# A four-layer graph network on one core: earlier loads at the end of layer 0, and layer 3's W2 products in pairs of 64 rows with the bias written by ScalarE

## The chip, the core and the metric

The kernel runs on one core of one Trainium2 chip, as one launch. The metric is the device time of one execution in microseconds; several executions are timed, and the median is given. The engines are TensorE (PE, with its weight loads PEld), VectorE (DVE), ScalarE (ACT), GpSimd (POOL) and SyncE (SP). SP issues the ordinary DMA transfers, POOL the indirect ones (gathers).

## What is computed

There are 8192 nodes with 32 features, and 262144 edges, sorted by target. Four layers follow each other, each one `x = layernorm(x + layer(x))`.

```
layer 0: w_e = weight[edge_type]            # 64 relations, 32x32 each
         out = segment_sum(x[src] @ w_e, dst)
layer 1: out = segment_sum(x[src] * edge_weight, dst)
layer 2: out = segment_sum(x[src], dst)
layer 3: h = relu(edge_attr_32 @ W1 + b1)   # 64 wide
         w = (h @ W2 + b2).reshape(E, 4, 8, 8)
         messages from x[src], edge_attr_4 and w, then segment_sum over dst,
         plus a product of each node's own x with si_w0 and si_w1
```

## The kernel before

The order of every engine's work is written out by hand in `raw_layers`. A `Flow` wraps an engine; `X.after(marks)` makes engine X wait for marks of other engines, `X.mark(ins)` makes one. All engines work in their program order, so an instruction that waits holds up all that stands behind it on its engine.

**Layer 0** walks over 256 groups `g` of eight tiles of 128 edges. POOL gathers rows of a table of products (`fetch_rows`, line 454), 12 groups ahead of their use and held to PE's marks; DVE splits the rows into three bf16 parts (`parts`, 806 to 811); PE adds them up by one-hot matrices (845). Beside it the loop does work for later layers. `matrices` builds 256 pieces of the dense matrices of layers 1 and 2 (PE line 654, in pairs of 64 rows; ACT 658 and 659) and stores them to DRAM (`amat` for layer 1, `cmat`, one byte per count, for layer 2). The last piece is made at group 207. `layer1(g)` multiplies such matrix pieces, loaded again by SP (`load1`, 695), with the node blocks that layer 0 has normalized already (715). A plan places 224 of the 256 products of layer 1 beside layer 0. The 32 that need the last block of nodes are left for layer 1's tail.

**Layer 1's tail** runs over `c` from 0 to 31: eight matmuls on a matrix piece of 1 MB (715), ACT's copy (724), a turn back by a small product (937), and a normalization for every fourth `c`. There are six buffers for the pieces. `pump` loads three of the 32 before layer 0 ends; the other loads wait for the end of layer 0 or for a buffer. The first 4 MB of layer 2's counts (`bring(0)`, 886) are loaded behind the first loads of the tail, and `widen(0, range(3))` turns them to bf16 at c = 16, split over DVE, ACT and POOL (965).

**Layer 2** has 16 such pieces of counts, each with 64 matmuls (1009).

**Layer 3** walks over 512 quads `q` of four tiles. POOL gathers four tiles per quad from the table `xtab`, eight quads ahead: `fetch_rows(q + AHEAD)` waits for the W2 products of quad q. Once for every two quads, `hidden(q + 2)` makes `h` for both: two matmuls with 32 rows of weights (1146), and two ACT instructions with Relu, one for each quad (1154), to a buffer of 65 rows whose last row is one. Then PE makes the W2 products of quad q (1170, 65 rows, so that the bias comes with the product) into one of two PSUM buffers, and then the sums of quad q - 4 (1179). DVE multiplies w with the gathered rows (1207, 1210, 1214), and its last product frees the PSUM buffer (`w_free`). So PE's order for two quads is: hidden, W2, sums, W2, sums.

Of the kernel before, what the change touches and what calls it, by code (L numbers as in the profile page):

```python
# [13 lines left out]
BF = mybir.dt.bfloat16  # L14
I32 = mybir.dt.int32
AF = mybir.ActivationFunctionType
# [5 lines left out]
P = 128  # L22
N = 8192
E = 262144
D = 32
# [10 lines left out]
GG = TT // GT  # L36
# [112 lines left out]
CB = 256  # L149
# [4 lines left out]
NC1 = 32  # L154
# [3 lines left out]
U8 = mybir.dt.uint8  # L158
# [45 lines left out]
def raw_layers(tc, x, a, w0, w1, b1, w2, si, m, bad):  # L204
    nc = tc.nc
    PE, V, A, G, S = (Flow(tc, e, n) for e, n in ((nc.tensor, "pe"), (nc.vector, "dve"), (nc.scalar, "act"),
                                                  (nc.gpsimd, "pool"), (nc.sync, "sp")))
# [32 lines left out]
    def now(f):  # L240
        return (f.sem, f.n)
# [9 lines left out]
    cut = Carve()  # L251
# [430 lines left out]
    def slot_of(n):  # L682

        r = n - n_in
        if r < 3:
            return 3 + n % 3, n - 3
        order = [3 + (n_in + k) % 3 for k in range(3)] + [0, 1, 2]
        return order[r % 6], (n - 6 if r >= 6 else None)

    def load1(n, *more):  # L690

        c, z = items[n]
        k, before = slot_of(n)
        S.after(stored[8 * c + 6], stored[8 * c + 7], used1.get(before), *more)
        land1[n] = m_ld[k].add(S.e.dma_start(slot1[k], amat[c // 16][c % 16, z, 0:P * 2048].rearrange("(p w) -> p w", w=2048)))

    def pump():

        while loaded[0] < len(items) and loaded[0] < n_in + 3:
            n = loaded[0]  # L700
            c, z = items[n]
            if made < 8 * (c + 1) or (n >= 3 and n - 3 not in used1):
                break
            load1(n)
            loaded[0] += 1

    def products(n, acc, first, last):
# [47 lines left out]
    def layer1(g):  # L755
# [11 lines left out]
            turned.append((c, h, h, take(sums1[:, h], bank[:, 6, 256 * h:256 * (h + 1)], pm, sums1_free[h])))  # L767
        pump()


    NS = TT // WT
    NO = 4
# [53 lines left out]
    for g in range(GG + 2):  # L826
        if g >= 2 and (g - 2) % per == per - 1:
            vm = bank_out((g - 2) // per)
            while done < NB // LC and ready(done) <= g - 1:
                acc = bank[:, (g - 2) // per % 2, 0:LC * D]  # L830
                agg_free[(g - 2) // per % 2] = vm = normalize(0, done, acc, windows(done, acc, (vm,)), x_a, x_b)
                normed[done] = ln_last[0]
                done += 1
        if g >= GG:
            continue
        h, bk, c = g % NO, (g // per) % 2, g % per
        if g == FIRST // 2:
            V.after(slots(), x_in)
        V.after(oh_free[h])
        pairs(oh[:, h], P, rel_b[:, g * GT:(g + 1) * GT])  # L840
        PE.after(parts(g))
        if c == 0:
            PE.after(agg_free[bk])
        for t in range(GT):
            ins = PE.e.matmul(bank[:, bk, 3 * c * D:3 * (c + 1) * D], oh[:, h, t // 2, :, t % 2],  # L845
                              xp[:, g % 4, t].rearrange("p c f -> p (c f)"), start=(t == 0), stop=(t == GT - 1))
        oh_free[h] = sums_of[g] = PE.mark(ins)
        turn_back()
        fetch_rows(g + AHEAD, 0, sums_of[g])
        if g >= FIRST:  # L850
            upto = min(CB, (g - FIRST + 1) * CB // SP1)
            while made < upto:
                matrices(made)
                made += 1
        add_up()
        fetch_rows(g + AHEAD, 1, now(PE))
        layer1(g)


    cut = Carve(33792)  # L860
    x3 = cut(NB, 3 * D, dt=BF)
    sums = cut(2, 512)
# [10 lines left out]
    for c in range(NC1):  # L873
        if c not in begun1:
            V.e.memset(y1[:, 2 * c:2 * c + 2, :], 0.0)
    cast = {}
    c_ld = [Landing(tc, f"ld_cm{k}") for k in range(2)]
    land = {}

    u8 = [arena[:, k:k + 8192].bitcast(U8) for k in (0, 16384)]  # L880
    ring = [arena[:, k:k + 4096].bitcast(BF) for k in (8192, 12288, 29696, 24576)]

    def bring(c, *free):
        if c < 16:
            S.after(*(cast[c - 2][-1] if c >= 2 else free))
            land[32 + c] = c_ld[c % 2].add(S.e.dma_start(u8[c % 2].rearrange("p (i w) -> p i w", w=2048),
                                                         cmat[16 * c:16 * (c + 1)].rearrange("i p w -> p i w")))

    while loaded[0] < min(len(items), n_in + 6):
        load1(loaded[0], *end)  # L890
        loaded[0] += 1
    bring(0, *end)
    G.after(*end)
    PE.after(ln_last[0], acc_free[0])
    sum_bank = [None, None]
# [50 lines left out]
                normed2[c * nb // LC] = ln_last[0]  # L946

    normed2 = {}
    ring_free = [None] * 4
    SHARE = (0, 48, 104, 128)  # L950

    def widen(c, ks=range(4)):

        if c >= 16:
            return
        cast.setdefault(c, [])
        v = u8[c % 2].rearrange("p (u r) -> p u r", r=256)
        for k in ks:
            o = ring[k].rearrange("p (u r) -> p u r", r=64)
            ms = []  # L960
            for e, F in enumerate((V, A, G)):
                us = slice(SHARE[e], SHARE[e + 1])
                F.after(land[32 + c], ring_free[k])
                src_, dst_ = v[:, us, 64 * k:64 * (k + 1)], o[:, us, :]
                ms.append(F.mark(F.e.activation(dst_, src_, AF.Copy) if F is A else F.e.tensor_copy(dst_, src_)))  # L965
            cast[c].append(ms)

    n = n_in
    for c in range(NC1):
        b = c % 2  # L970
        PE.after(sum_bank[b])
        for e in range(got[c], NQ1):
            pm = products(n, bank[:, b, 0:256], e == got[c], e == NQ1 - 1)
            if n + 6 < len(items):
                load1(n + 6)
            n += 1
        sum_bank[b] = am = take(sums[:, b, 0:256], bank[:, b, 0:256], pm, sum_free[b])
        if pend:
            turn(*pend)
        pend = (1, c, c, am)  # L980
        if c == NC1 // 2:
            widen(0, range(3))
    bring(1, pm)
    turn(*pend)
    ring_free[3] = pm
# [50 lines left out]
    w1_s = cut(64)  # L1036
    b1_s = cut(1)
    w2_s = cut(256)
    hs = cut(4, 512)
    ef = cut(3, 2, 512)  # L1040
    sh = cut(3, WT, 4)
    a0 = cut(2, WT, 16)
# [19 lines left out]
        c_ld.add(S.e.dma_start(w1_s[q * D:(q + 1) * D, :], w1))  # L1062
    for h in range(2):
        c_ld.add(S.e.dma_start(b1_s[64 * h:64 * h + 64], b1))
    c_in = c_ld.add(S.e.dma_start(w2_s[0:65], w2))
    for k in range(4):
        hm = V.mark(V.e.memset(hs[64:65, k], 1.0))

    e_ld = [Landing(tc, f"ld_ef{k}") for k in range(3)]
    s_ld = [Landing(tc, f"ld_sh{k}") for k in range(3)]  # L1070
# [50 lines left out]
    fetch(2)  # L1121
    PE.after(*free)
    A.after(*free)
    A.after(c_in, hm)

    h_free = None
    w_free = [zf[0], zf[1]]
# [11 lines left out]
    def hidden(q):  # L1139

        s = q // 8
        k = s % 3
        PE.after(batch[s]["e"], quad.get(q - 1, {}).get("h", h_free))
        for h in range(2):
            r = q % 4 + h
            ins = PE.e.matmul(bank[64 * h:64 * h + 64, 2, :], w1_s[r * D:(r + 1) * D, :],  # L1146
                              ef[r * D:(r + 1) * D, k, (q % 8) // 4, :], start=True, stop=True,
                              tile_position=(r * D, 64 * h))
        pm = PE.mark(ins)
        if q % 8 == 6:  # L1150
            ef_free[k] = pm
        for h in range(2):
            A.after(pm, quad.get(q + h - 4, {}).get("w"))
            quad[q + h] = dict(h=A.mark(A.e.activation(hs[0:64, (q + h) % 4], bank[64 * h:64 * h + 64, 2, :], AF.Relu,  # L1154
                                                       bias=b1_s[64 * h:64 * h + 64])))

    for q in range(AHEAD):
        fetch_rows(q)
    factors(0)
    PE.after(c_in, *zf)  # L1160
    hidden(0)
    for q in range(NQ + LAG3 + 2):

        if q % 2 == 0 and q + 2 < NQ:
            hidden(q + 2)
        if q < NQ:
            k, wp = w_bank()
            PE.after(quad[q]["h"], w_free[k])
            for t in range(4):
                ins = PE.e.matmul(wp[:, t, :], hs[0:65, q % 4, t * P:(t + 1) * P], w2_s[0:65], start=True, stop=True)  # L1170
            quad[q]["w"] = PE.mark(ins)
            quad[q]["k"] = k, wp
            fetch_rows(q + AHEAD)
# [58 lines left out]
        if 0 <= c < NQ and c % 2 == 1:  # L1232
            g = c // 2
            V.after(quad[c]["a"])
            V.e.tensor_reduce(win[:, g, 0:8], bank[:, g % 2, 0:128].rearrange("p (o k) -> p o k", k=16), AX.X, OP.add)
            rm = V.mark(V.e.tensor_reduce(r1, bank[:, g % 2, 128:320].rearrange("p (mo i) -> p mo i", i=8), AX.X, OP.add))
            V.after(rm)
            gm = V.mark(V.e.tensor_tensor(win[:, g, 8:].rearrange("p (o m) -> p o m", m=3),
                                          bank[:, g % 2, 320:344].rearrange("p (o m) -> p o m", m=3),
                                          r1.rearrange("p (m o) -> p o m", o=8), op=OP.add))  # L1240
            agg_free[g % 2] = gm
            while done < NB // LC and ready(done) <= g + 1:
                k, wp = w_bank()
                acc = bank[:, 3 + 2 * k, 0:LC * D]
                w_free[k] = normalize(3, done, acc, windows(done, acc, (w_free[k], gm)), z, x_a)
                done += 1


# [469 lines left out]
```

## Time and profile before

| | |
|---|---|
| median of 11 runs | 5797.4 us (5791.28 to 5806.86) |
| the profiled execution, its own time | 5799.02 us |
| its span from first to last instruction | 5797.3 us |
| mean granted TensorE clock | 0.886 |
| busy share PE, DVE, ACT, POOL | 82%, 76%, 33%, 71% |
| layer 0's last gather ends | 2805.0 us |
| layer 1's tail, first product to last turn | 2819.1 to 2923.3 us |
| layer 2's products | 2929.2 to 3172.9 us |
| layer 3's first gather starts, last gather ends | 3181.6 us, 5752.8 us |

The span holds almost the whole of the time. Its two long stages are layer 0 and layer 3; between them lie 377 us from the last gather of the one to the first of the other. Busy time is a mean over stages of different kinds, so each stage is read by itself. The granted clock is 1.00 or 0.50 in any short stretch; a mean between them is a mixture.

### The profile page before, as it was taken

The numbers are of one execution on the slowest core, as the hardware profiler recorded it, in microseconds if no ns is written. First come the engines' busy times: TensorE is split into PE (matmuls) and PEld (weight loads), VectorE is DVE, ScalarE is ACT, GpSimd is POOL, SyncE is SP. The second block draws the span as 40 slices with busy tenths as digits, with TensorE's granted clock in tenths as the row PEclk, the third lists the DMA queues.
The fourth block names the chain that finished last, engine by engine and source line by source line (L and its number), as shares of the span: only waits on it lengthen the run. The fifth ranks groups of instructions, "written<-read, shape, count | busy, mean of one in ns | idle before, by whom it ended". The sixth has DMA issues, their size and how long they took to land.

```text
span 5797.3 us, 89080 instructions
## 1 busy us (share of the span) xinstructions
PE 4730.8 (82%) x34726; PEld 3367.2 (58%) x34726; DVE 4411.4 (76%) x9512; ACT 1887.1 (33%) x3061; POOL 4142.1 (71%) x4238
## 2 busy tenths in 40 slices
PE   7456777777777787734499999999999999999998
PEld 3156666666666666522255566666666666666665
DVE  4269898989989898543356788888888878888886
ACT  5265555555555555200177111111111111111110
POOL 2677777777777777777256777777777777777775
PEclk7568888989999899756589899999999999999999
DMA  9636666769789899935576111111111111111111
GB/s 350 214 109 198 189 211 223 252 228 322 252 295 319 274 351 326 353 119 183 219 259 220 25 29 30 26 30 30 26 30 26 30 30 26 30 26 30 26 30 22
DMA packets 583102, 865.29 MB, mean 149 GB/s; under 512 B 102605, under 2 KB 441614, under 8 KB 549134
## 3 DMA queue, kind: packets, MB, share of 16 engines
q1 hardware_dynamic: 448094, 782.68, 38.3%
q0 software_dynamic: 134144, 73.67, 6.6%
q8 instruction: 275, 4.51, 0.3%
q10 hardware_dynamic: 432, 3.15, 0.2%
q14 instruction: 157, 1.29, 0.1%
HBM read 454.28 MB, written 404.88 MB: 148 GB/s over the span
## 4 chain that ended last, share of the span: by engine, by line
PE 25%; POOL 12%; DMA 6%; issue 4%; DVE 4%; ACT 0%; POOLq 0%; SPq 0%; DVEq 0%
POOL f_arena L454 12%; PE bank L1179 10%; PE bank L1170 8%; DMA f_arena<-fxtab,f_src 6%; PE bank L1009 4%; PE bank L1146 2%; DVE f_arena L1214 1%; PE bank L575 1%; PE bank L715 1%; PE bank L937 1%; DVE f_arena L1210 0%; DVE f_arena L588 0%; DMA f_arena<-famat 0%; DVE f_arena L1112 0%; DVE f_arena L1110 0%
## 5 line engine op out<-in xcount | busy, mean ns | idle before, releaser
L454 POOL DMA_INDIRECT f_arena<-fytab,f_row x2048 | 1957.7, 956 | 652.4 <-issue 541.0
L454 POOL DMA_INDIRECT f_arena<-fxtab,f_src x2048 | 1947.4, 951 | 643.6 <-issue 522.3
L654 PE MATMUL bank<-f_arena 64*128 64x128 f32 x16384 | 1196.7, 303 | 405.8 <-DVE f_arena L643 277.5
L654 PEld LDWEIGHTS bank<-f_arena 64*128 64x128 f32 x16384 | 1101.3, 210 | 485.8 <-DVE f_arena L643 304.4
L1179 PE MATMUL bank<-f_arena 128*128 128x344 f32 x4096 | 1309.6, 462 | 0.0
L1170 PE MATMUL bank<-f_arena 65*128 65x256 f32 x4096 | 1019.5, 392 | 68.3 <-DVE f_arena L1214 68.1
L1154 ACT ACTIVATE f_arena<-bank,f_arena 64x512 f32<-64x512 f32 x512 | 350.8, 685 | 2109.6 <-PE bank L1146 2103.2
L1170 PEld LDWEIGHTS bank<-f_arena 65*128 65x128 f32 x4096 | 768.3, 193 | 420.1 <-DVE f_arena L1214 127.5
L1179 PEld LDWEIGHTS bank<-f_arena 128*128 128x128 f32 x4096 | 798.1, 195 | 358.3 <-issue 29.6
L658 ACT ACTIVATE f_arena<-bank 128x512 uint8<-128x512 f32 x1024 | 613.1, 599 | 840.3 <-PE bank L654 729.6
L659 ACT ACTIVATE f_arena<-bank 128x512 f32<-128x512 f32 x1024 | 611.9, 598 | 0.0
L640 DVE TENSOR_TENSOR f_arena<-bank,f_arena 128x2048 f32<-128x2048 bf16 x256 | 586.5, 2291 | 8.7
L1214 DVE TENSOR_TENSOR f_arena<-bank,f_arena 128x256 f32<-128x256 f32 x1536 | 553.0, 418 | 0.0
L845 PE MATMUL bank<-f_arena 128*128 128x96 bf16 x2048 | 152.2, 226 | 335.2 <-DVE f_arena L811 335.1
L1110 DVE TENSOR_TENSOR f_arena<-f_arena 128x192 f32<-128x192 f32 x256 | 92.2, 360 | 396.5 <-DMA f_arena<-fxtab,f_src 394.2
L715 PE MATMUL bank<-f_arena,f_x_b 128*32 128x256 f32 x4096 | 314.3, 447 | 74.5 <-DMA f_arena<-famat 56.8
L845 PEld LDWEIGHTS bank<-f_arena 128*128 128x128 bf16 x2048 | 110.9, 108 | 417.8 <-DVE f_arena L811 330.5
L1210 DVE TENSOR_TENSOR f_arena<-bank,f_arena 128x512 f32<-128x512 f32 x512 | 349.8, 683 | 0.0
L588 DVE TENSOR_TENSOR f_arena<-bank,f_rel 128x512 f32<-128x512 f32 x512 | 349.3, 682 | 0.0
L638 DVE TENSOR_TENSOR f_arena<-bank,f_arena 128x1024 f32<-128x1024 bf16 x256 | 312.3, 1220 | 14.1 <-PE bank L654 11.9
L643 DVE TENSOR_TENSOR f_arena<-f_arena,bank 128x1024 f32<-128x1024 f32 x256 | 309.8, 1210 | 0.0
L965 POOL CAST f_arena<-f_arena 128x1536 bf16<-128x1536 uint8 x64 | 169.0, 2654 | 187.8 <-PE bank L715 75.9
(146 smaller groups left out, 4427.1 us busy)
## 6 DMA issues: line engine op xcount, KB each, us to landing
famat<-f_arena SPq DMA_DIRECT2D x256, 1024.0 KB
f_arena<-famat SPq DMA_DIRECT2D x256, 1024.0 KB, 11.7
fytab<-f_arena SPq DMA_DIRECT2D x64, 1024.0 KB, 11.9
fcmat<-f_arena SPq DMA_DIRECT2D x256, 256.0 KB
f_arena<-fcmat SPq DMA_DIRECT2D x16, 4096.0 KB, 14.8
f_arena<-fytab,f_row POOLq DMA_INDIRECT x2048
f_arena<-fxtab,f_src POOLq DMA_INDIRECT x2048
f_arena<-laid_ea SPq DMA_DIRECT2D x64, 512.0 KB, 3.5
```

Source lines behind the costliest of these rows:

```text
L454: return G.e.indirect_dma_start(out=dest, out_offset=None, in_=table, in_offset=bass.IndirectOffsetOnAxis(ap=ix, axis=0))
L588: return V.e.tensor_tensor(o, iota[:, None, :].to_broadcast([P, n, P]), rel[:, t:t + n, None].to_broadcast([P, n, P]), op=OP.is_equal)
L640: V.e.tensor_tensor(oh_l[:, b], iota2[:, None, :, 0].to_broadcast([P, 16, P]), meta_l[:, pp, k0:k0 + 16, None].to_broadcast([P, 16, P]), o ...
L654: ins = PE.e.matmul(two[:, h].rearrange("p (c s j) -> p c s j", s=64, j=4)[:, :, :, j], oh_l[hs_, b, 4 * q + j, :], oh_k[hs_, b, 4 * q + j ...
L658: A.e.activation(st_c[:, b, q], two[:, :, 0:256], AF.Copy)
L659: pair_free[u] = am = A.mark(A.e.activation(st_a[:, b, :, q].rearrange("p z h w -> p h z w"), two[:, :, 256:512].rearrange("p h (z w) -> p ...
L715: ins = PE.e.matmul(acc[q * D:(q + 1) * D, :].rearrange("p (u h j) -> p u h j", h=2, j=4), x_b[:, 8 * z + s, :], mv[:, s], start=(first an ...
L1154: quad[q + h] = dict(h=A.mark(A.e.activation(hs[0:64, (q + h) % 4], bank[64 * h:64 * h + 64, 2, :], AF.Relu, bias=b1_s[64 * h:64 * h + 64])))
L1170: ins = PE.e.matmul(wp[:, t, :], hs[0:65, q % 4, t * P:(t + 1) * P], w2_s[0:65], start=True, stop=True)
L1179: ins = PE.e.matmul(bank[:, g % 2, 0:MW], oh[:, c % NO, t, :], p[:, c % NP, t, :], start=(c % 2 == 0 and t == 0), stop=(c % 2 == 1 and t = ...
L1210: V.e.tensor_tensor(pq[:, :, 0:128].rearrange("p t (o k) -> p t o k", k=16), wp[:, :, 0:128].rearrange("p t (o k) -> p t o k", k=16), a0[: ...
L1214: ins = V.e.tensor_tensor(pq[:, :, 128 + 64 * mm:192 + 64 * mm].rearrange("p t (o i) -> p t o i", i=8), wp[:, :, 192:256].rearrange("p t ( ...
```

## The change

The change has two parts.

**Loads moved into layer 0.** When the last piece of the matrices is made (group 207), two of the tail's pieces are loaded into buffers 0 and 1, which `matrices` has used until then, and `bring(0)` loads the first counts into buffers that are dead as well. `pump` may now load five of the tail's pieces before the end of layer 0, the other three in the buffers of the planned ones. From four groups later on, eight ACT copies, one per group, turn two of the four parts of the first counts to bf16. A third part is done at c = 0 of the tail by the three engines together, in place of all three at c = 16; the fourth stays where it was.

**Layer 3's W2 products.** `h` now has both quads side by side on 2 x 64 partitions, made by one ACT instruction; W2 lies twice, on partitions 0 to 63 and 64 to 127, and each quad's four products run in an order that alternates the two halves. The bias row is gone: for each quad ACT writes the bias into the PSUM buffer first, as soon as DVE has freed it, and the products add to it. Identity products of the bias (`written`) are new too: four at the beginning of layer 3, and one behind each of the eight window sums, ahead of its normalization.

```diff
     def slot_of(n):
         r = n - n_in
-        if r < 3:
+        if r < 0:
             return 3 + n % 3, n - 3
-        order = [3 + (n_in + k) % 3 for k in range(3)] + [0, 1, 2]
-        return order[r % 6], (n - 6 if r >= 6 else None)
+        order = [0, 1] + [3 + (n_in + k) % 3 for k in range(3)] + [2]
+        return order[r % 6], n - 6 if r >= 6 else n - 5 if 2 <= r < 5 else None
...
+    def early_counts(g):
+        k = g - soon[0]
+        if k == 0:
+            ring_free[0] = ring_free[1] = now(PE)
+            for n in (n_in, n_in + 1):
+                load1(n, stored[CB - 2], stored[CB - 1])
+            bring(0, now(V), stored[CB - 1])
+        elif 4 <= k < 12:
+            q, u = (k - 4) // 4, slice((k - 4) % 4 * 32, (k - 4) % 4 * 32 + 32)
+            A.after(land[32], ring_free[q])
+            am = A.mark(A.e.activation(ring[q].rearrange("p (u r) -> p u r", r=64)[:, u],
+                                       u8[0].rearrange("p (u r) -> p u r", r=256)[:, u, 64 * q:64 * (q + 1)], AF.Copy))
...
         layer1(g)
+        if made == CB and soon[0] is None:
+            soon[0] = g
+        if soon[0] is not None:
+            early_counts(g)
...
     while loaded[0] < min(len(items), n_in + 6):
         load1(loaded[0], *end)
         loaded[0] += 1
-    bring(0, *end)
...
-        if c == NC1 // 2:
-            widen(0, range(3))
+        if c == 0:
+            widen(0, [2])
...
-    c_in = c_ld.add(S.e.dma_start(w2_s[0:65], w2))
-    for k in range(4):
-        hm = V.mark(V.e.memset(hs[64:65, k], 1.0))
+        c_ld.add(S.e.dma_start(w2_s[64 * h:64 * h + 64], w2[0:64, :]))
+    c_in = c_ld.add(S.e.dma_start(b2_s, w2[64:65, :].to_broadcast([P, 256])))
...
-        for h in range(2):
-            A.after(pm, quad.get(q + h - 4, {}).get("w"))
-            quad[q + h] = dict(h=A.mark(A.e.activation(hs[0:64, (q + h) % 4], bank[64 * h:64 * h + 64, 2, :], AF.Relu,
-                                                       bias=b1_s[64 * h:64 * h + 64])))
+        A.after(pm, quad.get(q - 3, {}).get("w"))
+        hm = A.mark(A.e.activation(hs[:, q // 2 % 2], bank[:, 2, :], AF.Relu, bias=b1_s))
+        quad[q] = dict(h=hm)
+        quad[q + 1] = dict(h=hm)
+
+    def written(b, c0):
+        return PE.e.matmul(bank[:, b, c0:512].rearrange("p (r c) -> p r c", c=256), ident,
+                           b2_s[:, None, :].to_broadcast([P, 2 - c0 // 256, 256]), start=(c0 == 0), stop=True,
+                           skip_group_check=True)
+
+    def biases(k, wp):
+        A.after(w_free[k])
+        return A.mark(A.e.activation(wp, b2_s[:, None, :].to_broadcast([P, 4, 256]), AF.Copy))
...
         if q % 2 == 0 and q + 2 < NQ:
             hidden(q + 2)
         if q < NQ:
             k, wp = w_bank()
-            PE.after(quad[q]["h"], w_free[k])
-            for t in range(4):
-                ins = PE.e.matmul(wp[:, t, :], hs[0:65, q % 4, t * P:(t + 1) * P], w2_s[0:65], start=True, stop=True)
+            PE.after(quad[q]["h"], biases(k, wp))
+            for t in (0, 2, 1, 3):
+                hp, c0 = slice(32 * (t & 2), 32 * (t & 2) + 64), 256 * (q % 2) + t % 2 * P
+                ins = PE.e.matmul(wp[:, t, :], hs[hp, q // 2 % 2, c0:c0 + P], w2_s[hp], start=False, stop=True,
+                                  skip_group_check=True)
...
-                w_free[k] = normalize(3, done, acc, windows(done, acc, (w_free[k], gm)), z, x_a)
+                windows(done, acc, (w_free[k], gm))
+                w_free[k] = normalize(3, done, acc, PE.mark(written(3 + 2 * k, 256)), z, x_a)
```

The host lays `edge_attr_32` out in another order to match.

More of the change, by code (lines that the diff above doesn't have):

```diff
@@ L697, in pump @@
     def pump():
-        while loaded[0] < len(items) and loaded[0] < n_in + 3:
+        while loaded[0] < n_in + 5:
             n = loaded[0]
             c, z = items[n]
-            if made < 8 * (c + 1) or (n >= 3 and n - 3 not in used1):
+            before = slot_of(n)[1]
+            if made < 8 * (c + 1) or (before is not None and before >= 0 and before not in used1):
                 break
-            load1(n)
+            if n not in land1:
+                load1(n)
             loaded[0] += 1
@@ L768, in layer1, with bring, widen @@
         pump()
+    cast = {}
+    c_ld = [Landing(tc, f"ld_cm{k}") for k in range(2)]
+    land = {}
+    u8 = [arena[:, k:k + 8192].bitcast(U8) for k in (0, 16384)]
+    ring = [arena[:, k:k + 4096].bitcast(BF) for k in (8192, 12288, 29696, 24576)]
+    def bring(c, *free):
+        if c < 16:
+            S.after(*(cast[c - 2][-1] if c >= 2 else free))
+            land[32 + c] = c_ld[c % 2].add(S.e.dma_start(u8[c % 2].rearrange("p (i w) -> p i w", w=2048),
+                                                         cmat[16 * c:16 * (c + 1)].rearrange("i p w -> p i w")))
+    ring_free = [None] * 4
+    SHARE = (0, 48, 104, 128)
+    def widen(c, ks=range(4)):
+        if c >= 16:
+            return
+        cast.setdefault(c, [])
+        v = u8[c % 2].rearrange("p (u r) -> p u r", r=256)
+        for k in ks:
+            o = ring[k].rearrange("p (u r) -> p u r", r=64)
+            ms = []
+            for e, F in enumerate((V, A, G)):
+                us = slice(SHARE[e], SHARE[e + 1])
+                F.after(land[32 + c], ring_free[k])
+                src_, dst_ = v[:, us, 64 * k:64 * (k + 1)], o[:, us, :]
+                ms.append(F.mark(F.e.activation(dst_, src_, AF.Copy) if F is A else F.e.tensor_copy(dst_, src_)))
+            cast[c].append(ms)
+    def early_counts(g):
[10 more added lines that the diff above has]
+                                       u8[0].rearrange("p (u r) -> p u r", r=256)[:, u, 64 * q:64 * (q + 1)], AF.Copy))
+            if k % 4 == 3:
+                cast.setdefault(0, []).append([am])
+    soon = [None]
     NS = TT // WT
@@ L857, in raw_layers @@
         layer1(g)
+        if made == CB and soon[0] is None:
+            soon[0] = g
+        if soon[0] is not None:
+            early_counts(g)
+    assert soon[0] + 12 < GG
     cut = Carve(33792)
@@ L875, in raw_layers @@
             V.e.memset(y1[:, 2 * c:2 * c + 2, :], 0.0)
[L876 to L887, printed above, removed]
     while loaded[0] < min(len(items), n_in + 6):
@@ L948, in raw_layers @@
     normed2 = {}
[L949 to L966, printed above, removed]
     n = n_in
@@ L1038, in raw_layers @@
     w2_s = cut(256)
-    hs = cut(4, 512)
+    b2_s = cut(256)
+    hs = cut(2, 512)
     ef = cut(3, 2, 512)
@@ L1123, in raw_layers @@
     A.after(*free)
-    A.after(c_in, hm)
+    A.after(c_in)
     h_free = None
@@ L1161, in raw_layers @@
     hidden(0)
+    for b in range(3, 7):
+        ins = written(b, 0)
+    w_free[:] = [PE.mark(ins)] * 2
     for q in range(NQ + LAG3 + 2):
@@ L1704 @@
     laid["ea4"] = arrays["ea4"].reshape(TT, P, 4).transpose(1, 0, 2).reshape(P, TT * 4)
-    laid["ea32"] = arrays["ea32"].reshape(P, 4, 512, D).transpose(1, 3, 0, 2).reshape(P, P, 512)
+    laid["ea32"] = arrays["ea32"].reshape(P, 2, 2, 2, 256, D).transpose(1, 3, 5, 0, 2, 4).reshape(P, P, 512)
     arrays = {f"in_{k}": np.ascontiguousarray(v) for k, v in arrays.items()}
```

## The prediction

> **What bounds the kernel now.** I read the page's costliest groups first, then the chain of waits between the layers, then PE's timeline and the granted clock in layer 3.
>
> The groups (line, engine, shapes, count; then busy time, mean ns, idle time before):
>
> ```profile
> L454 POOL DMA_INDIRECT f_arena<-fxtab,f_src x2048 | 1947.4, 951 | 643.6 <-issue 522.3
> L1179 PE MATMUL bank<-f_arena 128*128 128x344 f32 x4096 | 1309.6, 462 | 0.0
> L1170 PE MATMUL bank<-f_arena 65*128 65x256 f32 x4096 | 1019.5, 392 | 68.3 <-DVE f_arena L1214 68.1
> ```
>
> Layer 3's 2048 gathers run from 3181.6 to 5752.8 us: 1.2555 us each, busy 0.95 and a gap of 0.30 that is there with nobody to wait for. So POOL bounds layer 3: two quads (eight gathers) take 10.04 us. Layer 0's gathers run the same way, so work added or moved inside layer 0 costs nothing until PE falls 12 groups behind.
>
> The chain between the layers (start, duration, what):
>
> ```profile
> 2819.42 8.40 DMA f_arena<-famat
> 2833.61 10.17 DMA f_arena<-famat
> 2874.57 9.24 ACT f_arena L965 x3
> ```
>
> PE waits in layer 1's tail for matrix loads that start late, and for ACT while it widens counts.
>
> PE's timeline in layer 3, two rounds of two quads, the first with a wait:
>
> ```profile
> 4703.60 1.07 PE L1146 MATMUL bank<-f_arena 32*64 32x512 f32 x4
> 4706.13 1.99 PE L1170 MATMUL bank<-f_arena 65*128 65x256 f32 x8 [1.45 <-DVE f_arena L1214]
> 4707.96 4.17 PE L1179 MATMUL bank<-f_arena 128*128 128x344 f32 x8
> 4711.97 1.89 PE L1170 MATMUL bank<-f_arena 65*128 65x256 f32 x8
> 4713.69 2.48 PE L1179 MATMUL bank<-f_arena 128*128 128x344 f32 x8
> 4716.11 1.07 PE L1146 MATMUL bank<-f_arena 32*64 32x512 f32 x4
> 4717.11 2.00 PE L1170 MATMUL bank<-f_arena 65*128 65x256 f32 x8
> 4718.94 2.48 PE L1179 MATMUL bank<-f_arena 128*128 128x344 f32 x8
> 4721.27 1.89 PE L1170 MATMUL bank<-f_arena 65*128 65x256 f32 x8
> 4723.00 2.48 PE L1179 MATMUL bank<-f_arena 128*128 128x344 f32 x8
> 4725.41 1.07 PE L1146 MATMUL bank<-f_arena 32*64 32x512 f32 x4
> ```
>
> Without a wait a round takes 4716.11 to 4725.41 = 9.30 us, 0.74 below POOL's 10.04: PE is close behind. After the wait of 1.45 us the sums take 4.17 in place of 2.48, because the clock falls (stretch; busy PE, PEld, DVE, ACT, POOL; clock):
>
> ```profile
> 4704.62:4708.03 3.41, 1.96 (x11) 1.69 (x10) 3.34 (x11) 1.37 (x2) 2.52 (x3) 1.00 0.10 19
> 4708.03:4711.45 3.42, 3.42 (x8) 2.02 (x7) 3.27 (x11) 0.00 (x0) 2.51 (x4) 0.51 0.05 10
> ```
>
> All changes of the clock lie on one grid of 3.413 us, and one stretch at half clock loses half of it, 1.7 us. From 3240 to 5760 us I count 38 waits between hidden and W2 at full clock: of 13 below 1.2 us 4 were followed by half clock, of 12 between 1.2 and 1.6 us 6, of 13 from 1.65 us up all 13.
>
> **The loads, part by part.** The tail takes 2819.1 to 2923.3 = 104.2 us. PE's waits in it: 0.8 + 2.4 + 10.2 + 1.1 us for loads, 9.6 for ACT: 24. After the change five pieces lie ready, the 4 MB of counts no longer run in front of the other loads, and ACT widens one part (9.33 / 3 = 3.1 us) rather than three. This one sits behind the first copy, so turn 1 waits at most 1.8 us. DVE's share (5.09 / 3 = 1.7) and POOL's (4.28 / 3 = 1.4) hold up nobody: the first normalization comes at c = 3. Two ends: at half clock throughout (2.86 us for each c, timeline) 32 x 2.86 + 1.9 = 93.4 us, gain 11; at full clock (1.6 us) the loads bound it: 27 pieces of 1.05 MB are left at the end of layer 0, at the 419 GB/s of 2840 to 2880 us 2.50 us each, 67.6 + 4 for the first landing and the last product: 71.6, gain 33. The clock was mixed here before and will be: 22.
>
> The rest hides. On SP the early loads wait for the last stores and stand in front of the planned ones, some 30 us (12.5 us passed at 2821 behind the same 4 MB, the stores some 10, the two pieces 5). PE then was 6 groups behind its gathers (2396 us), POOL allows about 11, and 30 us is 3 groups; without that cover each group costs 10 us. The eight ACT copies (2048 elements; 512 take 0.60, 3584 take 3.17: 1.9 us) lie where ACT is busy 10 of 200 us.
>
> **Layer 3, part by part.** Removed: one Relu of two (0.70 us), half of W2's time on PE, four memsets. Added: a bias copy per quad, and a new order of waits. ACT works in order: Relu for q + 2, bias q, bias q + 1. Relu q + 2 waits for hidden q + 2, which is PE's instruction right before W2 of q. So W2 of q waits for hidden, Relu and bias in sequence, in every round, and behind it on PE stand the sums of q - 4 and all that follows. The sum:
> - hidden 1.07; ACT starts 0.06 later (4704.73); Relu 0.70 (two took 1.40); the bias, 1024 elements (256 take 0.41, 512 0.60, 3584 3.17): 0.98 to 1.04, I take 1.00; back to PE 0.07. A wait of 1.83 us.
> - W2 in pairs: no row has it; bounds are 0.5 and 1.0 of its 1.73. Layer 0's products of 64 rows in the same order take 2.06 us for 32 instructions of 128 columns, 0.064 each; W2's 256 columns take 0.216, so 0.108 for 128. That is 0.60: 1.04 us, the nearest row.
> - sums 2.41 each, as ahead of a hidden (2.33 ahead of W2).
>
> A round at full clock: 1.07 + 1.83 + 2 x 1.04 + 2 x 2.41 = 9.80, below 10.04. But the wait of 1.83 belongs to the class that dropped the clock 13 times of 13. A drop costs 1.7, and 0.24 / 1.7 = 0.14 drops per round are enough to make PE the bound. The products behind the new wait are denser (W2 in 1.04, not 1.99), so a stretch refills sooner: I take one drop in every two rounds, between none and one in each. 9.80 + 0.85 = 10.65; (10.65 - 10.04) x 256 rounds = 156 us. With one each: 11.50, 374 us.
>
> [...]
>
> Small: the four identity products at layer 3's start (at most 2 us each) end before DVE's first use at 3204; the one behind the last window sum adds 0.3 at the end. The other ACT work is hidden: some 1.0 x 512 more, ACT was 14% busy there. DVE (8.1 of 10.04 busy) has the other quad's work between freeing a buffer and its next use.
>
> **The sum.** 5799.0 (profiled) - 22 + 156 + 0.3 = 5933; the median lies 1.6 below: 5931.
>
> **The rivals.** *The gathers stay the bound* (12%): PE at 9.80 with hardly a drop; layer 3 as before, 5797.4 - 22 = 5775, faster. For it: POOL's steady 1.2555. It decides below 0.14 drops per round. *The rhythm locks* (23%): three stretches of 3.413 are 10.24 us; without a drop a round is shorter, with one longer, so PE may settle at a mean of 10.24: + 51, 5826. *A drop in every round* (15%): + 374, 6149. *W2 does not pair* (3%): a round of 11.2 even at full clock, 6070 to 6500. What I forecast, a drop in a third to four fifths of the rounds, 5850 to 6080, has 47%.
>
> **How the numbers follow.** The likeliest case gives 5931. The range goes from 5810 (the lock with the loads' best case is 5797 + 51 - 33 = 5815) to 6160 (a drop in each round, 6149); it leaves out the first rival, the case without pairs and a little on both sides, some 0.19. A measurement of this kernel can tell 0.2%, 12 us, from no change. Faster 0.12 is the first rival; same 0.04, a rhythm between the first two rivals; slower 0.84, all the rest.
>
> **What would show it.** Right: POOL's gathers in layer 3 over 1.27 us each with waits on PE; a wait of 1.7 to 2.0 us before W2 put down to ACT in each round; the clock in layer 3 well below 0.97; the tail at 72 to 93 us with no DMA wait of 10 us. Wrong: gathers at 1.2555, or a W2 group far from 1.04, or a bias far from 1.0 us.

## The result, and the profile after

The changed kernel takes 5894.9 us (median; 5889.9 to 5896.2) against 5797.2 for the kernel before: a ratio of 1.0167, 95% interval 1.0158 to 1.0175, 98 us slower. The profiled execution has a span of 5899.8 us, 102.5 more than before. Kernels e1 to e4 ran on a chip where the kernel before takes 5800.9 us; on the chips of the other eight runs every kernel, the one before too, takes over a quarter longer (7371 to 7415 us), with engines that stand idle for microseconds after what they waited for is done (in e12 a Relu starts at 6012.08, 4.27 us after the end of its hidden; in the changed kernel one starts at 4705.97, 0.05 us after), so those times are compared only with each other.

The page's groups after (same columns as before; hidden is now L1170, Relu L1177, the bias L1190, W2 L1209, the sums L1219, the identity products of the bias L1183):

```profile
L454 POOL DMA_INDIRECT f_arena<-fxtab,f_src x2048 | 1944.1, 949 | 748.7 <-issue 570.2
L1219 PE MATMUL bank<-f_arena 128*128 128x344 f32 x4096 | 1366.3, 476 | 0.0
L1209 PE MATMUL bank<-f_arena 64*128 64x256 f32 x4096 | 636.6, 433 | 465.4 <-ACT bank L1190 465.4
L1190 ACT ACTIVATE bank<-f_arena 128x1024 f32<-128x1024 f32 x512 | 505.3, 1022 | 12.7 <-DVE f_arena L1254 12.7
```

A gather costs POOL what it did (949 ns), but POOL stands idle 105 us longer. W2's own time fell from 1019 to 637 us, and in front of it stand 465 us of waiting for ACT's bias, where there were 68. From 3400 to 5600 us POOL's waits (us in total, times, longest) have a line that says who holds it now, the second below; the first is the same line before the change:

```profile
POOL f_arena L454 <- PE bank L1170: 9.4, 31, 0.3
POOL f_arena L454 <- PE bank L1209: 135.1, 113, 7.5
```

PE is the bound. Its timeline over one round:

```profile
4704.85 1.07 PE L1170 MATMUL bank<-f_arena 32*64 32x512 f32 x4
4707.63 1.13 PE L1209 MATMUL bank<-f_arena 64*128 64x256 f32 x8 [1.71 <-ACT bank L1190]
4708.69 2.59 PE L1219 MATMUL bank<-f_arena 128*128 128x344 f32 x8
4711.21 1.14 PE L1209 MATMUL bank<-f_arena 64*128 64x256 f32 x8
4712.27 2.59 PE L1219 MATMUL bank<-f_arena 128*128 128x344 f32 x8
4714.79 1.07 PE L1170 MATMUL bank<-f_arena 32*64 32x512 f32 x4
```

From one hidden to the next are 9.94 us at full clock. From 3240 us on I sorted all rounds: 194 of 9.95 us, 47 in which a stretch at half clock falls, 11.48 on average, and seven of 19.5 to 20.4 in which a window is normalized. Without the seven the mean is 10.244 us. Three stretches of the clock's grid are 10.240.

The grid fits the whole of layer 3: all 56 falls to half clock from 3240 us on, the first at 3252.53 and the last at 5887.62, lie within 0.001 us of one grid of 3.41333 us. It also shows which waits brought half clock (stretch; busy PE, PEld, DVE, ACT, POOL; granted clock, DMA share, GB/s):

```profile
3300.32:3303.73 3.41, 1.97 (x8) 0.50 (x6) 1.52 (x6) 1.40 (x2) 2.50 (x4) 1.00 0.07 13
3303.73:3307.14 3.41, 3.15 (x10) 2.02 (x11) 3.11 (x11) 1.16 (x2) 2.79 (x3) 0.50 0.09 14
...
3313.97:3317.38 3.41, 1.95 (x11) 1.36 (x12) 2.63 (x8) 2.36 (x3) 2.57 (x3) 1.00 0.43 149
3317.38:3320.79 3.41, 3.41 (x17) 1.96 (x16) 3.34 (x12) 0.00 (x0) 2.73 (x3) 1.00 0.09 15
```

PE is busy 1.97 us in the first stretch and 1.95 in the third, each with 1.45 us of a wait. After the first the clock falls, after the third it does not. The first one's busy time holds all of hidden, 1.07 us on 32 rows of weights; the third's is W2 and sums. Over all rounds of this trace there are 248 stretches at full clock that hold the whole of hidden: the 47 in which PE is busy for 1.97 us or less were all followed by half clock, and none of the 201 with 1.98 us or more was. By their place in the round, those 47 ended 2.52 to 2.81 us after a hidden began, the others at most 2.51 us after. Of the stretches without hidden, 17 have 1.95 to 1.97 us, and none of them was followed by half clock.

Before the change, when W2 ran on 65 rows, the clock fell after busier stretches too. This one of before (same columns) holds hidden's 1.07 us, 1.73 of W2 and a wait of only 0.59; half clock followed:

```profile
3718.25:3721.66 3.41, 2.82 (x13) 1.73 (x13) 3.34 (x11) 1.37 (x2) 2.77 (x3) 1.00 0.07 14
```

In the changed kernel this makes a rhythm. A round of 9.95 moves the grid's lines, the ends of its stretches, 0.29 us later in the round, until one reaches 2.52 us; the clock falls, the round takes 1.5 longer and the line jumps back. Such rounds begin at 3362.38, 3413.73, 3465.01 and 3516.25 us, and their falls come at 3365.17, 3416.37, 3467.57 and 3518.77 us, 51.20 apart. That is 15 stretches for five rounds, four of 9.95 and one of 11.4 to 11.6.

A round with a normalization (lines of PE and ACT taken out of the timeline):

```profile
3881.47 3.26 PE L575 MATMUL bank<-f_arena,f_shift 128*128 128x256 f32 x14 [0.38 <-DVE f_arena L1278]
...
3884.57 0.59 PE L1183 MATMUL bank<-f_arena,f_ident 128*128 128x256 f32 x2
...
3886.78 0.42 ACT L532 ACTIVATE f_lnf<-f_lnf 128x256 f32<-128x256 f32 x1 [9.39 <-DVE f_lnf L530]
...
3887.68 0.30 ACT L534 ACTIVATE f_lns<-f_lns,f_small 128x8 f32<-128x8 f32 x1 [0.49 <-DVE f_lns L533]
3887.89 1.01 ACT L1190 ACTIVATE bank<-f_arena 128x1024 f32<-128x1024 f32 x1
...
3888.95 2.08 PE L1209 MATMUL bank<-f_arena 64*128 64x256 f32 x8 [3.79 <-ACT bank L1190]
```

The bias of the odd quad stands behind the normalization's two steps on ACT, and W2 waits 3.79 us for it and then runs at half clock. The round takes 20.42, 10.4 more than POOL's 10.04. Before, such rounds were nearly as long (14.6 to 21.1, the seven 134.6 together; now 142.0), but PE's rounds of 9.30 made it good.

The sum, from the two profiles: layer 3 starts 20.0 us sooner (first gather 3161.55 for 3181.55); 241 x (10.244 - 10.04) = 49; the seven rounds 142.0 - 7 x 10.04 = 72. Together +101, of 102.5 measured.

Layer 1's tail, PE at its loads:

```profile
2882.22 1.07 PE L717 MATMUL bank<-f_arena,f_x_b 128*32 128x256 f32 x16 [0.87 <-DMA f_arena<-famat]
...
2884.72 1.07 PE L717 MATMUL bank<-f_arena,f_x_b 128*32 128x256 f32 x16 [0.87 <-DMA f_arena<-famat]
```

It takes 78.1 us (2824.3 to 2902.4), 26.1 less. The load wait of 10 us and ACT's 9 us are gone; where the clock is full, PE meets the loads, one each 2.5 us.

### The profile page after: what moved, and what is told of

Read it like the earlier page. It is cut to its first block, busy times and chain, and to the rows that moved or that the text cites. A ratio compares the mean times of both kernels' runs of the same rounds, so it can differ in the third digit from the quotient of the medians.

```text
span 5899.8 us, 89563 instructions
## 1 busy us (share of the span) xinstructions
PE 4479.6 (76%) x34750; PEld 2934.0 (50%) x34750; DVE 4416.0 (75%) x9506; ACT 2200.3 (37%) x3323; POOL 4143.6 (70%) x4236
## 4 chain that ended last, share of the span: by engine, by line
PE 43%; ACT 7%; DVE 1%; issue 1%; POOL 1%; DMA 0%; DVEq 0%; ACTq 0%
PE bank L1219 22%; PE bank L1209 10%; PE bank L1170 4%; ACT bank L1190 4%; PE bank L1033 4%; ACT f_arena L1177 3%; PE bank L717 1%; PE bank L980 1%; PE bank L575 1%; POOL f_arena L454 1%; DMA f_arena<-famat 0%; DVE f_arena L1254 0%; DVE f_lnf L530 0%; DVE f_lnf L525 0%; DVE f_lns L533 0%
## 5 line engine op out<-in xcount | busy, mean ns | idle before, releaser
L1219 PE MATMUL bank<-f_arena 128*128 128x344 f32 x4096 | 1366.3, 476 | 0.0
L654 PEld LDWEIGHTS bank<-f_arena 64*128 64x128 f32 x16384 | 1102.8, 210 | 489.6 <-DVE f_arena L643 313.2
L1219 PEld LDWEIGHTS bank<-f_arena 128*128 128x128 f32 x4096 | 760.3, 196 | 513.6 <-issue 215.4
L1209 PE MATMUL bank<-f_arena 64*128 64x256 f32 x4096 | 636.6, 433 | 465.4 <-ACT bank L1190 465.4
L1177 ACT ACTIVATE f_arena<-bank,f_arena 128x512 f32<-128x512 f32 x256 | 176.5, 690 | 1958.5 <-PE bank L1170 1958.5
L1209 PEld LDWEIGHTS bank<-f_arena 64*128 64x128 f32 x4096 | 381.2, 201 | 844.8 <-ACT bank L1190 694.5
L1247 DVE TENSOR_TENSOR f_arena<-bank,f_arena 128x256 f32<-128x256 f32 x512 | 215.9, 422 | 491.0 <-PE bank L1209 491.0
L1254 DVE TENSOR_TENSOR f_arena<-bank,f_arena 128x256 f32<-128x256 f32 x1536 | 552.6, 417 | 0.0
L1190 ACT ACTIVATE bank<-f_arena 128x1024 f32<-128x1024 f32 x512 | 505.3, 1022 | 12.7 <-DVE f_arena L1254 12.7
## 6 DMA issues: line engine op xcount, KB each, us to landing
f_arena<-fcmat SPq DMA_DIRECT2D x16, 4096.0 KB, 14.6
```

What stands on the lines that cost most here:

```text
L654: ins = PE.e.matmul(two[:, h].rearrange("p (c s j) -> p c s j", s=64, j=4)[:, :, :, j], oh_l[hs_, b, 4 * q + j, :], oh_k[hs_, b, 4 * q + j ...
L1177: hm = A.mark(A.e.activation(hs[:, q // 2 % 2], bank[:, 2, :], AF.Relu, bias=b1_s))
L1190: return A.mark(A.e.activation(wp, b2_s[:, None, :].to_broadcast([P, 4, 256]), AF.Copy))
L1209: ins = PE.e.matmul(wp[:, t, :], hs[hp, q // 2 % 2, c0:c0 + P], w2_s[hp], start=False, stop=True, skip_group_check=True)
L1219: ins = PE.e.matmul(bank[:, g % 2, 0:MW], oh[:, c % NO, t, :], p[:, c % NP, t, :], start=(c % 2 == 0 and t == 0), stop=(c % 2 == 1 and t = ...
L1254: ins = V.e.tensor_tensor(pq[:, :, 128 + 64 * mm:192 + 64 * mm].rearrange("p t (o i) -> p t o i", i=8), wp[:, :, 192:256].rearrange("p t ( ...
```

## Experiments

My theory after the result: the loads bring what was forecast; in layer 3 the wait in series makes PE the bound, its rounds are held at 10.24 us by the clock's grid, and the normalizations, which PE can no longer make good, cost the rest. The rivals: the wait costs as such and the clock is incidental; the new shape of W2 slows PE; the loads share in the loss.

**e1, the loads alone.** The diff up to layer 3, with layer 3 as before.

> The first half of the change alone: early loads in layer 0, one widened part in layer 1's tail, layer 3 as before. Theory (layer 1's tail is 26 us shorter, the end of layer 0 some 5 later, layer 3 starts 20 us sooner and runs as before, bound by the gathers): 5771 to 5779. Rival (the early loads also cost something inside layer 0 or layer 3, so that part of the changed kernel's loss is theirs): 5785 to 5810.

Measured: 5776.0 against 5800.9, ratio 0.9956 (0.9939 to 0.9972), 25 us less. The tail takes 84.1 us in its profile. The loads have no part in the loss.

**e2, layer 3 alone.** The rest of the diff, with the loads as before.

> The second half alone: paired W2 and ScalarE's bias in layer 3, the loads as before. Theory (the whole loss is layer 3's, 118 us, whatever comes before it): 5910 to 5920, rounds of 9.95 us with a half-clock stretch in one of about five, mean 10.24 without the normalizations. Rival (the loss hangs on the phase at which layer 3 meets the 3.413 us grid, or on the loads): below 5895 or above 5935.

Measured: 5917.8, ratio 1.0199 (1.0182 to 1.0216), 117 us more. There are 243 rounds with a mean of 10.242 us, 47 of them long, and seven with a normalization of 19.5 to 20.5: the same rhythm, though layer 3 starts 25 us later. It does not hang on the phase at the start.

**e3, the bias first.**

```
-        if q % 2 == 0 and q + 2 < NQ:
-            hidden(q + 2)
         if q < NQ:
             k, wp = w_bank()
+            bm = biases(k, wp)
+        if q % 2 == 0 and q + 2 < NQ:
+            hidden(q + 2)
+        if q < NQ:
-            PE.after(quad[q]["h"], biases(k, wp))
+            PE.after(quad[q]["h"], bm)
```

> The changed kernel with one thing moved: ScalarE writes the bias of an even quad before the Relu of the next pair, not after it, so that W2 of an even quad waits for nothing that hidden releases. Theory (the wait of 1.71 us in series is what made PE the bound): PE's round without a wait is 9.95 - 1.71 = 8.24 us, the gathers bound layer 3 again at 1.2555 us each, 10.04 a round: 5895 - 118 = 5777, between 5768 and 5785. Rival 1 (pairs and changes of tile shape are what slows PE): layer 3 stays at over 10.2 us a round, 5880 to 5900. Rival 2 (the wait is replaced by one for VectorE, which is late with the banks): 5800 to 5870.

Measured: 5774.5, ratio 0.9953 (0.9936 to 0.9969), 26 us less than before. Its PE timeline, and its POOL waits from 3300 to 5600 us:

```profile
4703.76 1.07 PE L1170 MATMUL bank<-f_arena 32*64 32x512 f32 x4
4704.77 1.13 PE L1211 MATMUL bank<-f_arena 64*128 64x256 f32 x8
4705.83 2.59 PE L1221 MATMUL bank<-f_arena 128*128 128x344 f32 x8
...
4711.93 1.07 PE L1170 MATMUL bank<-f_arena 32*64 32x512 f32 x4
```

```profile
POOL f_arena L454 <- PE bank L1211: 7.3, 24, 0.3
```

A round without a wait is 8.17 us, the shape of W2 and sums unchanged; POOL never stands longer than its usual 0.3 us; its 2048 gathers take 2575 us, 1.257 each. The order of two instructions on ACT was the whole loss. There are more stretches at half clock here (clock 0.94, in the changed kernel 0.96) and normalization rounds of 20 to 29 us, and neither costs anything, for POOL bounds. This version beats both kernels, by the loads' part: it equals e1.

**e4, work in the wait.**

```
+            bm = biases(k, wp)
+            if q % 2 == 0 and LAG3 <= q < NQ - 2:
+                u = (q - LAG3) // 2 % 2
+                PE.after(agg_free[u])
+                for _ in range(6):
+                    PE.e.matmul(bank[:, u, MW:512], ident, b2_s[:, 0:512 - MW], start=True, stop=True, ...)
-            PE.after(quad[q]["h"], biases(k, wp))
+            PE.after(quad[q]["h"], bm)
```

> The changed kernel with six products of the identity (168 columns, some 1.2 us, written to unused columns of a sum bank and read by nobody) between hidden and W2 of each even quad, inside the wait of 1.71 us. Theory (the clock, by its 3.413 us grid, sets the mean round of 10.24 us where the round at full clock is 9.95): no half clock after this wait, rounds of 9.95 to 10.04 us, the seven rounds with a normalization still some 9 us longer: (10.25 - 10.02) x 244 = 56 us less, or up to 70: 5825 to 5845. Rival (the wait itself costs the time and the clock is incidental): 5890 to 5900 with fewer drops, or longer if the filler delays W2.

Measured: 5855.7, ratio 1.0096 (1.0079 to 1.0112), 39 less than the changed kernel's 5894.9 (41 by the two ratios). PE's timeline and the clock over layer 3:

```profile
4707.31 1.07 PE L1170 MATMUL bank<-f_arena 32*64 32x512 f32 x4
4708.31 1.98 PE L1211 MATMUL bank<-f_arena,f_ident 128*128 128x168 f32 x12
4710.22 1.13 PE L1216 MATMUL bank<-f_arena 64*128 64x256 f32 x8
```

```profile
3240.00:5820.00 2580.00, 2549.03 (x12059) 1561.07 (x12057) 2051.57 (x6095) 641.09 (x760) 1874.04 (x1982) 0.99 0.14 27
```

No stretch at half clock follows a hidden any more, and 240 rounds have a mean of 10.075 us. The filler took 1.91 us, not 1.2, and so delays W2 by 0.13, which is why 5855 and not the expected 5825 to 5845: (10.244 - 10.075) x 241 = 41 less was to be had. The seven normalization rounds sum to 143.0 us, with 142.0 in the changed kernel. The rival that the clock is incidental is out: more work on PE made the kernel faster.

**e5 to e8, on a second chip** (the kernel before: 7415.1 us). e5 adds a copy of 128x8 elements between Relu and bias, to a new small buffer `xx`; e6 issues the odd quads' bias behind the W2 of the quad before them, ahead of the normalization; e7 does so for all quads; e8 has W2's order changed. In the lines below `ahead` starts empty, and the condition of e6 is written out.

```
e5:  +            if q % 2 == 0 and q + 2 < NQ:
     +                A.e.activation(xx, b2_s[:, 0:8], AF.Copy)
e6:  -            PE.after(quad[q]["h"], biases(k, wp))
     +            if q not in ahead:
     +                ahead[q] = w_bank()
     +                ahead[q] += (biases(*ahead[q]),)
     +            k, wp, bm = ahead[q]
     +            PE.after(quad[q]["h"], bm)
     ...
     +            if q + 1 < NQ and q % 2 == 0:      # e7: without q % 2 == 0
     +                ahead[q + 1] = w_bank()
     +                ahead[q + 1] += (biases(*ahead[q + 1]),)
     ...
     +                nxt[0] += 1                    # behind normalize
e8:  -            for t in (0, 2, 1, 3):
     +            for t in range(4):
```

> The changed kernel with one more small ScalarE copy (128x8 elements, read by nobody) between the Relu and the bias of each even quad, 256 in all; a ScalarE operation on 128x8 took 0.30 us in a normalization, so the wait grows from 1.71 to some 1.9 to 2.0 us and the full-clock round from 9.95 to some 10.15 to 10.24. Theory (the half-clock stretches lock the mean round to three stretches of the grid, 10.24 us, whatever the full-clock round is below it): fewer stretches at half clock, the same mean, 5885 to 5910. Rival (waits and stretches add up independently): 249 x 0.2 to 0.3 = 50 to 75 us more, 5945 to 5970.

> The changed kernel with the bias of odd quads issued one quad earlier, ahead of the normalization's ScalarE steps (the order of an even quad, Relu before bias, is kept; a normalization gives its own bank to the next quad). Theory (the seven rounds of 20.4 us lose 6.3 us each because the bias stands behind the normalization's two ScalarE steps and the clock falls in that wait of 3.8 us; the other rounds stay at a mean of 10.24): 7 x 6.3 = 44 less, 5851, between 5843 and 5862, rounds with a normalization of some 14 us. Rival (those rounds are absorbed in the lock or the stall comes back behind VectorE's normalization): 5880 to 5900.

> Every bias one quad earlier: the order of the run with the bias first, and the normalization's too. Theory (the gathers are the bound once no even W2 waits for hidden): no faster than with the bias first alone, 5768 to 5780, with fewer stretches at half clock. Rival (the normalizations' stalls of PE still cost time there): 10 to 40 us less, 5735 to 5765.

> The changed kernel with W2's four products in the order 0, 1, 2, 3, so that two neighbours use the same 64 rows; nothing else. Theory (products on different rows run beside each other, on the same rows one after the other): W2 takes 1.40 us if the middle two still overlap, 1.73 if none do, in place of 1.06; a full-clock round of 10.6 to 11.3, which no longer locks at 10.24, and with the stretches at half clock 6020 to 6230. The sums behind it, 2.52 with pairs, fall back to 2.41 if the change between pairs and whole rows is what costs 0.1, and stay at 2.52 if not. Rival (order does not matter): 5885 to 5905.

Measured: e5 7623.1 (1.0277 of before, 1.0258 to 1.0296), e6 7580.9 (1.0221, 1.0202 to 1.0241), e7 7400.1 (0.9978, 0.9968 to 0.9987), e8 7626.3 (1.0280, 1.0257 to 1.0303). Durations of PE's work at full clock are those of the first chip. In e8:

```profile
6032.82 1.14 PE L1209 MATMUL bank<-f_arena 64*128 64x256 f32 x8 [1.71 <-issue]
6033.89 2.59 PE L1219 MATMUL bank<-f_arena 128*128 128x344 f32 x8
```

W2 takes 1.07 us with neighbours on the same 64 rows as well, and the sums still 2.52. So what made W2 shorter is not that two products alternate between the halves. But pairs there are, in either order. Two very short stretches at the start of a W2 (same columns) show how many instructions PE has at once, one in the kernel before, two in e8:

```profile
4706.13:4706.15 0.02, 0.02 (x1) 0.02 (x1) 0.02 (x1) 0.00 (x0) 0.01 (x1) 1.00 0.00 0
6032.82:6032.84 0.02, 0.02 (x2) 0.02 (x2) 0.00 (x0) 0.02 (x1) 0.00 (x0) 1.00 0.00 0
```

Over the whole trace 2048 of the 4096 W2 instructions of the changed kernel start 7 ns (median) behind the one before, and in e8 2042 start 13 ns behind; before the change none does, and they follow each other 215 ns apart. Which two instructions make a pair is not in the trace. Since nothing else differs, e8 stands for the changed kernel on this chip. Beside it e6 is 45 us shorter, as expected (44). The seven rounds with a normalization take 118.7 us in e6's trace and 159.5 in e8's, while the mean of the others is 12.33 and 12.30. In e6 W2 follows the normalization's products without a wait:

```profile
6024.54 0.59 PE L1185 MATMUL bank<-f_arena,f_ident 128*128 128x256 f32 x2
6025.06 1.13 PE L1214 MATMUL bank<-f_arena 64*128 64x256 f32 x8
```

e7 is 226 below e8 and 0.2% below the kernel before: the order again. Whether it would beat e3 on the first chip was not run. e5 says little: the copy moved the bias by only 0.10 us. It is 3 us below e8, where the rival asks for 25 more, and the intervals of the two reach 14 and 17 us to each side.

**e9 to e12, two more chips.** e9 and e11 have two such copies, e10 and e12 are e6 once more.

> The changed kernel with two more small ScalarE copies (128x8 elements, read by nobody) between the Relu and the bias of each even quad. One of them moved the bias by 0.10 us in the run before, so the wait grows by 0.20 us to 1.91 and the full-clock round from 9.95 to 10.15 us, still under 10.24. Theory (the half-clock stretches hold the mean round at three stretches of the 3.413 us grid, whatever the full-clock round is below it): fewer stretches at half clock, the same mean outside the normalizations, 5885 to 5910. Rival (waits and stretches add up independently): 249 x 0.20 = 50 us more, 5935 to 5955.

> The same kernel as in the run with the odd bias ahead, on another chip. Theory (the seven rounds with a normalization lose 6.3 us each to the bias behind ScalarE's normalization steps; the other rounds keep their mean of 10.24): 5843 to 5862, rounds with a normalization of some 14 us. Rival (the stall comes back behind VectorE's normalization or is absorbed by the grid): 5880 to 5900.

> The kernel with two more small ScalarE copies in each even quad's wait once more, on another chip, since the chip of the run before was disturbed in every kernel. Theory (the grid holds the mean round at 10.24 us): 1.0155 to 1.0195 of the kernel before, the changed kernel's own 1.0167. Rival (0.20 us x 249 = 50 us more): 1.024 to 1.027.

> The kernel with the odd bias ahead of the normalization once more, for the same reason. Theory (7 x 6.3 = 44 us less than the changed kernel): 1.008 to 1.011 of the kernel before, rounds with a normalization of some 14 us. Rival (the stall comes back elsewhere): 1.014 to 1.017.

Measured: 7601.9 and 7556.9 on the third chip (before 7370.8), 7638.1 and 7571.7 on the fourth (before 7414.5). By ratio the expectations of e11 and e12, 1.0155 to 1.0195 and 1.008 to 1.011, were missed, and so were their rivals': 1.0294 and 1.0208. These chips break the rhythm: in e5, e6 and e8 only 36 to 39% of the rounds take 9.9 to 10.2 us, and the others up to 33. With the rhythm broken the grid's line falls anywhere in the round, and one thing can be counted: of 481 waits of 1.7 us that began at full clock (e6, e8, e10, e12) 125 were followed by half clock within a stretch, 26%; of 257 of 1.9 us (e9, e11) 95, 37%. e10 lies 45 below e9 and e12 66 below e11. In the traces the rounds with a normalization account for 48 and 36 of it (163.5 us against 115.9, 157.0 against 121.0). The mean of the other rounds is 12.38 in both e9 and e10, and 12.42 in e11 against 12.30 in e12: for the two copies that is nothing on one chip and some 30 us on the other, where the rival asked for 50. Whether the mean round stays at 10.24 when the wait grows is therefore open. What the first chip shows for it are two kernels with 10.244 and 10.242, and e4 without falls of the clock, and with a round longer at full clock, at 10.075.

## Why the prediction was right or wrong

The time, 5931 for 5895, and the direction were right; the way there was half right. That the total came within 36 us is in part luck: two errors largely took each other out, 107 us too much for the rounds and 72 left out for the normalizations.

- *Loads*: 22 taken, 26 measured in the tail, 20 at the start of layer 3, 25 in e1. The tail lay between the two ends (71.6 and 93.4), with loads 2.50 us apart at full clock and a wait of 1.55 for the widened part, at most 1.8 foretold. What hides: the eight copies took 1.90 us each; layer 0's last gather ends 5 us later than before, in e1 3 to 4: the cover held but for these.
- *The wait*: 1.71 for 1.83, in 249 rounds, put down to ACT's bias; Relu 0.69, bias 1.02. Right.
- *W2*: 1.06 for 1.04, right in size, from the nearest row. W2 runs in pairs, as taken; that its order has to alternate between the halves for this, which I believed until e8, is wrong.
- *Sums*: 2.52 each, not 2.41. This is the mis-sized term of the full-clock round: 2 x 0.11 more, 0.12 less for the wait and 2 x 0.02 more for W2 lift it to 9.94 from 9.80. The row of before was taken behind products of 65 rows; behind those of 64 rows the sums took 2.52 in either order of the halves, and no run here isolates why.
- *Falls of the clock*: 47 in 241 rounds, 0.20 each and not 0.5, at 1.53 us and not 1.7: 0.30 per round, not 0.85. This is the step that failed: "13 of 13" from 1.65 us up was a count of waits alone. In the changed kernel's trace the same wait left the clock alone when the stretch held no hidden (17 of 1.95 to 1.97 us), or held it with more than 1.97 us of busy PE (201). Before the change W2 on 65 rows, 1.73 us of the stretch at 3718.25 where W2 now takes 1.06, took the place of the sums in such stretches; the denser products behind the new wait, named as a reason to go below one, fit this, but no run isolates them. So the step gave 156 us where rhythm and rounds cost 49: the second rival, "the rhythm locks at 10.24" (+51), describes 241 of the 248 rounds, and I gave it 23%.
- *Left out*: the normalizations. I looked at what the change adds to them (0.3 us at the end) and not at ACT's order in them, nor at what had paid for them until then, PE's slack. 72 us.
- *What would show it*: POOL's gathers over 1.27 us each (1.305), a W2 wait of 1.7 to 2.0, a tail of 72 to 93 without a load wait of 10 us: all seen. A clock well below 0.97 was not: 0.96. That was the sign that the falls were fewer than forecast.

## What to carry to other kernels

Where an engine works in order, look at which of its instructions another engine waits for, and put those that need nothing new ahead of those that do: here one moved line was worth 120 us. When a change takes slack from an engine, list every rare stall (a normalization, a batch load) that this slack used to make good; here each of seven came to cost some 10 us. In this kernel a periodic wait had to be set against the grid of the clock together with what else lay in its stretch, not judged by its length.

## What was not expected of the hardware

The clock follows more than PE's busy time: stretches with 1.97 and 1.95 us busy had opposite ends, and the one that fell held 1.07 us of products with 32 rows. Before the change a stretch with 2.82 us busy fell, 2.80 of it products with 32 and 65 rows. One grid of 3.4133 us fits all falls in layer 3. A loop with a round a little under three of its stretches (9.95) settled at their length, 10.24, because a fall came back whenever a line reached the same place, 2.52 us or more after a hidden began; where no such fall came (e4, 10.075) it did not settle there, and the six idle products per round that kept the clock made the kernel 39 us faster. Fp32 products of 64 rows and 256 columns took 0.133 us an instruction (1.06 for eight), two starting nearly together, in either order of the halves, against 0.216 with 65 rows, one after the other. A 128x8 copy on ACT between two others moved the second by 0.10 us (e5), though an ACT instruction on 128x8 in a normalization took 0.30.
